# A graph attention layer on one core: the gathered rows weighted in place, one column group of PE per chunk, one gate per batch

## The chip, the cores and the metric

The kernel runs on one core of a Trainium2 chip. The time is that of one execution on the device, in microseconds (us); the figure for a kernel is the median of several runs. The profile is of one execution and has its own time, which stands beside its span below. The engines are PE (matrix multiply), DVE (vector), ACT (activations and copies), POOL (here the issuer of gathers) and SP (issuer of other DMAs).

## The reference

There are N = 12,500 nodes with 128 features and E = 412,500 edges, sorted by target, each with 64 features. `h` is the layer-normed, rectified `x`. For four heads of 32 columns:

```python
h = (node_features @ W_node.T).reshape(num_nodes, H, HD)
e = (edge_features @ W_edge.T).reshape(num_edges, H, HD)
att = jnp.sum(jnp.concatenate([h[src], h[tgt], e], -1) * a, axis=-1)
att = jnp.where(att > 0, att, 0.2 * att)
m = jnp.maximum(segment_max(att, tgt), 0.0)
ex = jnp.exp(att - m[tgt])
denom = segment_sum(ex, tgt) + (num_edges - deg)[:, None] * jnp.exp(-m)
h_prime = segment_sum((ex / denom[tgt])[:, :, None] * h[src], tgt)
return x + h_prime
```

So for every edge a row of `h` is fetched by its source, weighted by a softmax weight, and added up at its target.

## The kernel before, in words

A first stage, of some 112 us, makes a table of rows in HBM, one for each node. A row has `ROW` = 140 floats: four parts of the attention logit that depend on the source, four that depend on the target (`FH` = 8 in all), and for each head its 32 values of `h` and a one (`HB` = 33 floats). The columns come from one matrix, `wall`. For 128 nodes at a time, three such blocks together, ACT copies the product out of PSUM and ACT's queue writes it to the table (`keep_rows`).

The edges are cut into chunks of 896 (`CE`): seven tiles (`T`) of 128 edges, one edge per partition. Eight chunks (`CB`) make a batch, and there are 58 batches, the last with five chunks. Since the edges are sorted, the targets of one chunk lie in a window of 32 nodes (`W`), from the first target on. Per batch:

- `load` lets SP fetch the edge features (`eft`), the targets and eight small slices of the table (`twb`), and names the buffer `hs`, of which there are two, for 56 tiles of 128 rows.
- `gather` has POOL issue one indirect DMA for each of the 56 tiles: 128 rows of the table, chosen by `src`, go to `hs`. The tiles are taken in the order of t, for each t chunk by chunk.
- `weigh` takes the first four columns of `hs` by a stream transpose on DVE (`zst`), adds them to the logits in PSUM (`z`), finds the maximum in each segment by two scans, and leaves the weights `ex` and the maxima `mx` in PSUM, edges on partitions.
- `scatter` goes chunk by chunk. ACT copies `mx` into a buffer `rhs` (three take turns), DVE writes the product of the gathered values and `ex` into it, and PE multiplies it by `hot`, the 0/1 matrix of edge against target. Three tiles (`G` = 3) are done in one matmul, 96 rows of result by 420 columns, of which only the three diagonal blocks of 32 by 140 are wanted; the seventh tile is one of 32 by 140. The result `pa` has one bank for each of two chunks. `keep` lets ACT copy the three blocks to `pas` in SBUF, three copies per chunk, one chunk behind.
- `begin` prepares the next batch: the masks on DVE (`mem`, `key`, `hot`), and `z` on PE from the edge features and `twb`.
- `collect` adds the three blocks and turns them from (row) to (head, row) by partition, in four matmuls with `rsame`, and ACT copies the result into `r`.
- Every second batch, `merge` joins the sums of 16 chunks to the accumulator `acc` on DVE; where a part of the nodes is complete, `finish` divides and adds `x`, and SP stores it.

The order of all this is written out by hand: each engine follows the program's order. In turn b of the main loop come, one after another, `load` and the first part of `gather` for batch b + 1, then `weigh` and `scatter` of b, `begin` of b + 1, `collect` of b, and perhaps `merge` and `finish`. The gathers of b + 1 go into the buffer that batch b - 1 used. They are issued in three parts, cut by `STOPS = (0, 18, 37)`. Ahead of a part stands a gate: a copy of one column on POOL, from something that another engine writes.

```python
if sums is not None:
    nc.gpsimd.tensor_copy(gate[:sums.shape[0], :], sums)
```

The first part's gate reads `r` of batch b - 1. The other two are set inside `scatter`, by `follow`: after the sums of chunk 1, and after those of chunk 5, of batch b itself. (For the first batch there are no gates, and none ahead of the first part of the second.)

After the main loop a further stage, `window`, handles chunks whose targets do not fit one window. It is a loop whose count is worked out from the data.

Of the kernel before, what the change touches and what calls it, by code (L numbers as in the profile page):

```python
# [10 lines left out]
F32 = mybir.dt.float32  # L11
BF16 = mybir.dt.bfloat16
I32 = mybir.dt.int32
AF = mybir.ActivationFunctionType
OP = mybir.AluOpType
# [3 lines left out]
P = 128  # L19
# [4 lines left out]
H = 4  # L24
HD = D // H
T = 7
CE = T * P
CT = 2 * T
NCH = -(-E // CE)
LAST = -(-(E - (NCH - 1) * CE) // P)  # L30
SB = 4
# [5 lines left out]
G = 3  # L37
# [3 lines left out]
W = 32  # L41
NB = -(-N // P)
# [4 lines left out]
FH = 2 * H  # L47
HB = HD + 1
ROW = FH + H * HB
R = CB * H  # L50
NQT = P // R
STOPS = (0, 18, 37)
AW = HD + 3
BUF = max(CE, MC * 2 * AW, CB * H * AW)
# [5 lines left out]
def tiles_of(sc):  # L60

    return [T if c < NCH - 1 else max(LAST, G) for c in (2 * sc, 2 * sc + 1) if c < NCH]


def filled(sc):

    return [T if c < NCH - 1 else LAST for c in (2 * sc, 2 * sc + 1) if c < NCH]
# [23 lines left out]
def kernel(  # L91
# [61 lines left out]
    rhs_bufs = []  # L153
    for i in range(3):
        r = const.tile([P, T, H, AW], F32, name=f"rhs{i}")
        nc.gpsimd.memset(r[:, :, :, HD + 1:], 1.0)
        rhs_bufs.append(r)
# [16 lines left out]
    with (  # L174
# [36 lines left out]
        wall_h = wall[:, FH:].rearrange("p (h k) -> p h k", h=H)  # L211
        nc.vector.memset(wall, 0.0)
        nc.vector.tensor_copy(wall_h[:, :, :HD], pw.rearrange("p (h d) -> p h d", h=H))
        pa = pps.tile([P, FH], F32, name="pw", bufs=1)
        nc.tensor.matmul(pa, wn, a_diag[:, 0:2, :].rearrange("p j h -> p (j h)"), start=True, stop=True)
        nc.vector.tensor_copy(wall[:, :FH], pa)
# [97 lines left out]
        def keep_rows(u):  # L314
            nc.scalar.copy(u.rows, u.ph[:, :u.m, :])
            nc.vector.memset(u.rows[:, :, FH:].rearrange("p b (h k) -> p b h k", h=H)[:, :, :, HD], 1.0)
            nc.vector.tensor_copy(tn[:, u.b0:u.b0 + u.m, :], u.ph[:, :u.m, H:FH])
            if u.last:
                b0, n, rows = u.last
                nc.scalar.dma_start(table[b0 * P:(b0 + n) * P, :].rearrange("(b p) c -> p b c", p=P),  # L320
                                    rows[:, :n, :])
# [91 lines left out]
    def load(s):  # L413

        c0 = s.b * CB
        s.eft = work.tile([P, SB, CE], F32, name="eft")
        nc.sync.dma_start(s.eft, ef[s.b * SB:(s.b + 1) * SB, :, :].rearrange("j p e -> p j e"))
        s.mem = work.tile([P, 2, CE], F32, name="mem")
        for k in range(2):
            rows = dstc[c0 + 4 * k:c0 + 4 * k + 4, :]  # L420
            nc.sync.dma_start(s.mem[:, k, :].bitcast(I32), rows[:, None, :].to_broadcast([4, W, CE]))
        _, at = nc.values_load_multi_w_load_instructions(
            least_i[0:1, c0:c0 + CB], engines=[ENG.SP], min_val=0, max_val=NB * P - W,
            skip_runtime_bounds_check_because="a dst is at most N, and N + W at most NB * P")
        for i, v in enumerate(at):
            r = (i % 4) * W
            nc.sync.dma_start(twb[r:r + W, s.b % 2, i // 4, i * H:(i + 1) * H], table[ds(v, W), H:FH])
        s.hs = work.tile([P, SB * CT, ROW], F32, name="hs", bufs=2)
        s.tiles = []
        for t in range(T):  # L430
            for sc in range(s.b * SB, (s.b + 1) * SB):
                held = filled(sc) + [0, 0]
                for c in range(2):
                    i = (sc - s.b * SB) * CT + c * T + t
                    if t < held[c]:
                        s.tiles.append(i)
                    else:
                        nc.vector.memset(s.hs[:, i, :], 0.0)

    def gather(s, stop, sums=None):  # L440

        if sums is not None:
            nc.gpsimd.tensor_copy(gate[:sums.shape[0], :], sums)  # L443
        i0 = STOPS[stop]
        i1 = STOPS[stop + 1] if stop + 1 < len(STOPS) else len(s.tiles)
        for i in s.tiles[i0:i1]:
            nc.gpsimd.indirect_dma_start(  # L447
                out=s.hs[:, i, :], out_offset=None, in_=table[:, :],
                in_offset=bass.IndirectOffsetOnAxis(ap=s.src[:, i:i + 1], axis=0))
# [39 lines left out]
    def weigh(s):  # L489
# [4 lines left out]
                            s.hs.rearrange("p (q t) k -> p t q k", t=T)[:, :, :, :H])  # L494
# [25 lines left out]
    def scatter(s, follow):  # L520


        last = None
        for j in range(SB):
            sc = s.b * SB + j
            for c, n in enumerate(tiles_of(sc)):
                q = 2 * j + c
                rhs = rhs_bufs[(2 * sc + c) % 3]
                nc.scalar.copy(rhs[:, :n, :, HD + 2], s.mx[:, :n, q * H:(q + 1) * H])  # L529
                i0 = j * CT + c * T  # L530
                nc.vector.tensor_tensor(  # L531
                    rhs[:, :n, :, :HB], s.hs[:, i0:i0 + n, FH:].rearrange("p t (h d) -> p t h d", h=H),
                    s.ex[:, :n, q * H:(q + 1) * H, None].to_broadcast([P, n, H, HB]), op=OP.mult)
                pa = ps.tile([P, G * H * AW], F32, name="pa", bufs=2)

                order = [*range(0, n - G, G), n - G] if n % G == 0 else [0, n - n % G, *range(G, n - n % G, G)]
                for i in order:
                    w = min(G, n - i)
                    nc.tensor.matmul(pa[:w * W, :w * H * AW],  # L539
                                     s.hot[j][:, c * T + i:c * T + i + w, :].rearrange("p t r -> p (t r)"),  # L540
                                     rhs[:, i:i + w, :, :].rearrange("p t h k -> p (t h k)"),
                                     start=(i == order[0]), stop=(i == order[-1]))
                if last is not None:
                    keep(s, *last)
                    if last[0] % 2:
                        follow(last[0] // 2)
                last = (q, pa)
        keep(s, *last)

    def keep(s, q, pa):  # L550
        for g in range(G):
            rows = slice(g * W, (g + 1) * W)
            nc.scalar.copy(s.pas[rows, q, :], pa[rows, g * H * AW:(g + 1) * H * AW])  # L553
# [3 lines left out]
    def collect(s):  # L557

        n = s.chunks
        t2 = ps.tile([P, CB, AW], F32, name="t2")  # L560
        for h in range(H):
            nc.tensor.matmul(t2[h * W:(h + 1) * W, :n, :], rsame[:G * W, :], s.pas[:G * W, :n, h * AW:(h + 1) * AW],
                             start=True, stop=True, tile_position=(0, h * W))
        k = s.b % MB
        if k == 0:
            merged["r"] = work.tile([P, AW, MC + 1], F32, name="r")
        at = 1 + k * CB
        nc.scalar.copy(merged["r"][:, :, at:at + n], t2[:, :n, :].rearrange("p c d -> p d c"))  # L568

    def merge(g, n):  # L570
# [34 lines left out]
        here = ps.tile([P, MC, 2], F32, name="t2")[:, :n, :]  # L605
# [15 lines left out]
    def count_windows():  # L621
# [13 lines left out]
        row = ps.tile([1, NC2], F32, name="t2")  # L635
# [72 lines left out]
    with tc.manual_schedule():  # L708
        for b in range(-1, NBT):
# [6 lines left out]
            if b + 1 < NBT:  # L716
                load(batch(b + 1))
                if b >= 1:
                    at = 1 + (b - 1) % MB * CB
                    gather(batch(b + 1), 0, merged["r"][:, 0, at:at + 1])  # L720
                else:
                    for k in range(len(STOPS) if b < 0 else 1):
                        gather(batch(b + 1), k)
            if b >= 0:
                s = batch(b)
                weigh(s)
                if b + 1 < NBT:
                    load_pen(batch(b + 1))
                for store in stores:
                    store()  # L730
                stores.clear()
                s.pas = work.tile([P, BUF], F32, name="m")[:, :CB * H * AW].rearrange("p (c k) -> p c k", c=CB)

                def follow(j):
                    if b + 1 < NBT and j in (0, 2):
                        gather(batch(b + 1), 1 + j // 2, s.pas[:G * W, 2 * j + 1, 0:1])

                scatter(s, follow)
# [21 lines left out]
    def window():  # L760
# [59 lines left out]


# [44 lines left out]
        for c in range(2):  # L866
            nc.vector.tensor_tensor(z[:, c * T:(c + 1) * T, :], pzt[:, :, c * H:(c + 1) * H],
                                    hs[:, c * T:(c + 1) * T, :H], op=OP.add)
# [56 lines left out]
        for c in range(2):  # L925
            nc.scalar.activation(rhs_bufs[c][:, :, :, HD], att[:, c * T:(c + 1) * T, :], AF.Exp)
# [3 lines left out]
        for c in range(2):  # L930
            t = slice(c * T, (c + 1) * T)
            rhs = rhs_bufs[c]
            nc.vector.tensor_tensor(rhs[:, :, :, :HD],
                                    hs[:, t, FH:].rearrange("p t (h d) -> p t h d", h=H)[:, :, :, :HD],
                                    rhs[:, :, :, HD:HD + 1].to_broadcast([P, T, H, HD]), op=OP.mult)
            for i in range(T):
                k = i % 4
                nc.tensor.matmul(pa[k * W:(k + 1) * W, c, :], hot[:, c * T + i, :],
                                 rhs[:, i, :, :].rearrange("p h k -> p (h k)"),
# [62 lines left out]
```

## Time and profile before

| | |
|---|---|
| Median of three runs | 4299.8 us (4298.55 to 4304.43) |
| The profiled execution | 4299.55 us, its span 4297.8 us |
| Granted PE clock, mean | 0.693 of full speed |
| Busy: POOL | 3107.8 us, 72% |
| Busy: DVE, PE, ACT | 42%, 41%, 17% |
| First gather, last gather | start at 112.85, at 4239.94 us |
| HBM traffic | 417.15 MB read, 15.09 MB written |
| Gathers' queue | 103,136 packets, 231.23 MB, 20.9% of the 16 DMA engines' time |

Busy time is what an engine spent in instructions; the profile does not count registers, semaphores and the issuing of DMAs as busy. Each gather is one instruction on POOL. "Releaser" is what ended a stretch of idle time; "issue" means that nothing the profile shows did. In the names, `m<-pa` is the copy to `pas`, `exr` the bank of `ex` and `mx`, `t<-m,rsame` the matmuls of `collect`, `up` a bank that several steps use in turn.

### The profile page before, as it was taken

Reading aid. Unit: us, or ns where it says so; the run is one execution under the profiler, and the core shown is the slowest. Engines: PE = TensorE matmul, PEld = TensorE weight load, DVE = VectorE, ACT = ScalarE, POOL = GpSimd, SP = SyncE. Lnnn points to the kernel's source line nnn. Section 1 sums busy time; section 2 is a strip of 40 time slices with the busy share of each in tenths; the row PEclk is TensorE's granted clock in tenths of the full one; section 3 lists DMA queues with packets and bytes.
Section 4 is the critical chain, followed back from the end, with each engine's and each line's share of the span. In section 5 each row is a group of like instructions: output and inputs, shape, how many; then the busy total and the mean of one; then the engine's idle time right before and its main releaser. Section 6 shows DMA issues by size and latency. Waiting matters only on the chain.

```text
span 4297.8 us, 25217 instructions
## 1 busy us (share of the span) xinstructions
PE 1767.8 (41%) x5421; PEld 572.8 (13%) x5421; DVE 1788.9 (42%) x3449; ACT 746.4 (17%) x2606; POOL 3107.8 (72%) x3417
## 2 busy tenths in 40 slices
PE   6234344343434443434343434343434343434343
PEld 4011111111111111111111111111111111111111
DVE  7233443344333433443334334443343344433444
ACT  5011111111111111111111111111111111111111
POOL 2777777777777777777777777777777777777773
PEclk8576767676767676767676767676767676767676
DMA  5333433333333333333333333333333333333331
GB/s 159 108 110 84 123 94 110 89 114 85 114 89 109 94 109 89 113 85 114 89 110 93 110 89 112 87 114 90 109 94 109 90 113 85 112 91 110 93 110 36
DMA packets 243603, 434.17 MB, mean 101 GB/s; under 512 B 93914, under 2 KB 144086, under 8 KB 243446
## 3 DMA queue, kind: packets, MB, share of 16 engines
q0 software_dynamic: 103136, 231.23, 20.9%
q1 hardware_dynamic: 126486, 192.44, 13.8%
q10 hardware_dynamic: 13824, 8.82, 0.7%
q8 instruction: 47, 0.77, 0.1%
q14 instruction: 110, 0.90, 0.1%
HBM read 417.15 MB, written 15.09 MB: 101 GB/s over the span
## 4 chain that ended last, share of the span: by engine, by line
POOL 45%; issue 18%; DVE 14%; PE 9%; ACT 6%; DMA 5%; DVEq 0%; POOLq 0%; ACTq 0%
POOL hs L447 44%; PE pa L539 9%; DMA hs<-table,src 5%; DVE up L505 3%; DVE m L507 3%; ACT both L511 2%; DVE z L501 2%; ACT a L502 2%; DVE rhs L531 2%; DVE z L503 1%; DVE a L508 1%; DVE exr L517 1%; ACT m L553 1%; DVE zst L493 1%; POOL gate L443 0%
## 5 line engine op out<-in xcount | busy, mean ns | idle before, releaser
L447 POOL DMA_INDIRECT hs<-table,src x3223 | 3052.6, 947 | 1060.8 <-issue 1058.0
L539 PE MATMUL pa<-rhs,hot 128*96 128x420 f32 (+1 forms) x2762 | 1092.5, 519 | 2216.8 <-DVE rhs L531 2216.3
L531 DVE TENSOR_TENSOR rhs<-hs,exr 128x924 f32<-128x924 f32 x461 | 514.9, 1117 | 608.2 <-ACT rhs L529 608.2
L539 PEld LDWEIGHTS pa<-rhs,hot 128*96 128x96 f32 (+1 forms) x2762 | 333.3, 159 | 2968.6 <-issue 2693.8
L493 DVE STREAM_TRANSPOSE zst<-hs 128x224 f32<-128x224 f32 x58 | 23.9, 411 | 1356.2 <-DMA hs<-table,src 1356.2
L553 ACT COPY m<-pa 32x140 f32<-32x140 f32 x1383 | 367.3, 266 | 762.8 <-PE pa L539 752.1
L465 PE MATMUL z<-eft,wa 128*32 128x384 f32 (+1 forms) x928 | 361.6, 543 | 23.3 <-DMA twb<-table 23.3
L502 ACT ACTIVATE a<-z 32x224 f32<-32x224 f32 x232 | 80.3, 346 | 1539.2 <-DVE z L501 1539.2
L468 PE MATMUL z<-mem,twb 128*32 128x512 f32 x464 | 186.1, 544 | 5.1 <-DMA twb<-table 5.1
L511 ACT ACTIVATE both<-a 32x224 f32<-32x224 f32 x232 | 89.9, 388 | 375.0 <-DVE a L508 370.7
L465 PEld LDWEIGHTS z<-eft,wa 128*32 128x32 f32 x928 | 97.7, 110 | 283.0 <-issue 283.0
L684 PE MATMUL up<-a,ident 128*32 128x224 f32 (+2 forms) x480 | 45.2, 555 | 214.8 <-DVE a L677 214.8
L484 DVE TENSOR_TENSOR hot<-exr,key 128x448 f32<-128x448 f32 x231 | 128.1, 617 | 2.4 <-DVE key L477 0.5
L501 DVE TENSOR_TENSOR z<-z,zst 32x224 f32<-32x224 f32 x232 | 89.8, 387 | 79.9 <-ACT a L502 73.1
L619 DVE TENSOR_TENSOR acc<-acc,a 128x70 f32 x461 | 108.4, 235 | 34.6 <-DVE acc L619 19.8
L529 ACT COPY rhs<-exr 128x28 f32<-128x28 f32 x461 | 96.4, 209 | 132.3 <-DVE rhs L531 68.7
L507 DVE TENSOR_TENSOR_SCAN m<-pen,up 32x896 f32<-32x896 f32 x58 | 116.5, 2008 | 6.7
L505 DVE TENSOR_TENSOR_SCAN up<-pen,z 32x896 f32<-32x896 f32 x58 | 117.0, 2017 | 2.0
L568 ACT COPY r<-t 128x280 f32<-128x280 f32 (+1 forms) x58 | 23.7, 408 | 506.1 <-PE z L468 505.5
L580 DVE TENSOR_SCALAR mc<-r 128x16 f32<-128x16 f32 (+1 forms) x29 | 6.1, 209 | 229.3 <-ACT r L568 229.3
L513 DVE SCALAR_TENSOR_TENSOR both<-pen,m 32x224 f32<-32x224 f32 x232 | 90.2, 389 | 2.4
L460 DVE TENSOR_SCALAR mem<-mem,nid 128x896 f32<-128x896 int32 x116 | 74.7, 685 | 21.9 <-issue 16.2
(140 smaller groups left out, 1037.8 us busy)
## 6 DMA issues: line engine op xcount, KB each, us to landing
eft<-in_ef SPq DMA_DIRECT2D x58, 1792.0 KB
mem<-in_dstc SPq DMA_DIRECT2D x116, 448.0 KB
hs<-table,src POOLq DMA_INDIRECT x3223, 2.6
twb<-table SPq DMA_DIRECT2D x464, 0.5 KB
pen<-pens SPq DMA_DIRECT2D x58, 112.1 KB
table<-rows ACTq DMA_DIRECT2D x10, 630.0 KB
xg<-in_x SPq DMA_DIRECT2D x14, 448.0 KB
out<-xg SPq DMA_DIRECT2D x13, 448.0 KB
```

The costliest lines, as they stand in the source:

```text
L447: nc.gpsimd.indirect_dma_start(out=s.hs[:, i, :], out_offset=None, in_=table[:, :], in_offset=bass.IndirectOffsetOnAxis(ap=s.src[:, i:i + ...
L465: nc.tensor.matmul(s.z[:, part], wa3[:, j, :], s.eft[:, j, part], start=(j == 0), stop=False)
L468: nc.tensor.matmul(s.z[:, part], twb[:, s.b % 2, k, :], s.mem[:, k, part], start=False, stop=(k == 1))
L484: nc.vector.tensor_tensor(hot, rows_ps[:, None, :].to_broadcast([P, CT, W]), key[:, j * CT:(j + 1) * CT, None].to_broadcast([P, CT, W]), o ...
L501: nc.vector.tensor_tensor(grouped(s.z, g), grouped(s.z, g), zst[g * R:(g + 1) * R, :, :], op=OP.add)
L502: nc.scalar.activation(grouped(att, g), grouped(s.z, g), AF.Identity, scale=0.2)
L505: nc.vector.tensor_tensor_scan(up, s.pen[:, :CE], s.z, 0.0, op0=OP.add, op1=OP.max)
L507: nc.vector.tensor_tensor_scan(m[:, ::-1], s.pen[:, CE:0:-1], up[:, ::-1], 0.0, op0=OP.add, op1=OP.max)
L511: nc.scalar.activation(both[g * R:(g + 1) * R, 0, :, :], grouped(att, g), AF.Exp)
L531: nc.vector.tensor_tensor(rhs[:, :n, :, :HB], s.hs[:, i0:i0 + n, FH:].rearrange("p t (h d) -> p t h d", h=H), s.ex[:, :n, q * H:(q + 1) * ...
L539: nc.tensor.matmul(pa[:w * W, :w * H * AW], s.hot[j][:, c * T + i:c * T + i + w, :].rearrange("p t r -> p (t r)"), rhs[:, i:i + w, :, :].r ...
L553: nc.scalar.copy(s.pas[rows, q, :], pa[rows, g * H * AW:(g + 1) * H * AW])
```

## The change

The layout of the table changes: a row has, for each head, 32 values, two ones and the logit's source part (`AW` = 35 floats), then the four target parts: `EROW` = 140, `ROW` = 144. So a gathered row already has the shape of PE's operand. In `scatter`, ACT copies `mx` over the logit column of `hs`, for all chunks at first; DVE multiplies the first 33 columns of each head by `ex` in place; and PE takes `hs` itself as its moving operand, one tile of 140 columns at a time. Each chunk has a column group of PE, hence 32 partitions of the result, by its number modulo 4 (`G` is now 4); two chunks take turns. The result of all eight chunks is one bank, `s.pa`.

`keep`, `follow`, `rhs_bufs`, `STOPS` and the matmuls of `collect` are gone. `collect` instead has ACT move each group and head straight from PSUM to `r`, sixteen copies per batch. Ahead of these it writes one column, `sums`, which the only gate of a batch reads: the gathers of batch b + 1 are issued in one part, behind the end of PE's work for batch b - 1.

```diff
-G = 3
+G = P // W
-FH = 2 * H
-ROW = FH + H * HB
-STOPS = (0, 18, 37)
 AW = HD + 3
+HB = HD + 1
+EROW = H * AW
+ROW = EROW + H
...
-    rhs_bufs = []
-    for i in range(3):
-        r = const.tile([P, T, H, AW], F32, name=f"rhs{i}")
-        nc.gpsimd.memset(r[:, :, :, HD + 1:], 1.0)
-        rhs_bufs.append(r)
+    sums = const.tile([P, 1], F32, name="sums")
...
-            nc.vector.memset(u.rows[:, :, FH:].rearrange("p b (h k) -> p b h k", h=H)[:, :, :, HD], 1.0)
-            nc.vector.tensor_copy(tn[:, u.b0:u.b0 + u.m, :], u.ph[:, :u.m, H:FH])
+            nc.vector.memset(u.rows[:, :, :EROW].rearrange("p b (h k) -> p b h k", h=H)[:, :, :, HD:HD + 2], 1.0)
+            nc.vector.tensor_copy(tn[:, u.b0:u.b0 + u.m, :], u.ph[:, :u.m, EROW:])
...
-            nc.sync.dma_start(twb[r:r + W, s.b % 2, i // 4, i * H:(i + 1) * H], table[ds(v, W), H:FH])
+            nc.sync.dma_start(twb[r:r + W, s.b % 2, i // 4, i * H:(i + 1) * H], table[ds(v, W), EROW:])
...
-    def gather(s, stop, sums=None):
+    def gather(s, sums=None):
         if sums is not None:
-            nc.gpsimd.tensor_copy(gate[:sums.shape[0], :], sums)
-        i0 = STOPS[stop]
-        i1 = STOPS[stop + 1] if stop + 1 < len(STOPS) else len(s.tiles)
-        for i in s.tiles[i0:i1]:
+            nc.gpsimd.tensor_copy(gate, sums)
+        for i in s.tiles:
             nc.gpsimd.indirect_dma_start(
...
-                            s.hs.rearrange("p (q t) k -> p t q k", t=T)[:, :, :, :H])
+                            s.hs[:, :, :EROW].rearrange("p (q t) (h k) -> p t q h k", t=T, h=H)[:, :, :, :, AW - 1])
...
-    def scatter(s, follow):
+    def scatter(s):
+        s.pa = ps.tile([P, CB // G, H * AW], F32, name="pa", bufs=2)
+        by_chunk = s.hs[:, :, :EROW].rearrange("p (q t) (h k) -> p q t h k", t=T, h=H)
+        for q in range(s.chunks):
+            nc.scalar.copy(by_chunk[:, q, :, :, AW - 1], s.mx[:, :, q * H:(q + 1) * H])
         for j in range(SB):
+            tiles = list(enumerate(tiles_of(s.b * SB + j)))
+            for c, n in tiles:
+                q = 2 * j + c
+                rows = by_chunk[:, q, :n, :, :HB]
+                nc.vector.tensor_tensor(
+                    rows, rows, s.ex[:, :n, q * H:(q + 1) * H, None].to_broadcast([P, n, H, HB]), op=OP.mult)
+            for i in range(T):
+                for c, n in tiles:
+                    if i < n:
+                        q = 2 * j + c
+                        g = q % G
+                        nc.tensor.matmul(s.pa[g * W:(g + 1) * W, q // G, :], s.hot[j][:, c * T + i, :],
+                                         s.hs[:, q * T + i, :EROW],
+                                         start=(i == 0), stop=(i == n - 1), tile_position=(0, g * W))
...
     def collect(s):
         n = s.chunks
-        t2 = ps.tile([P, CB, AW], F32, name="t2")
-        for h in range(H):
-            nc.tensor.matmul(t2[h * W:(h + 1) * W, :n, :], rsame[:G * W, :], s.pas[:G * W, :n, h * AW:(h + 1) * AW],
-                             start=True, stop=True, tile_position=(0, h * W))
+        if s.b + 2 < NBT:
+            nc.scalar.copy(sums, s.pa[:, CB // G - 1, 0:1])
...
-        nc.scalar.copy(merged["r"][:, :, at:at + n], t2[:, :n, :].rearrange("p c d -> p d c"))
+        for g in range(min(n, G)):
+            to = merged["r"][:, :, at + g:at + n:G]
+            for h in range(H):
+                nc.scalar.copy(to[h * W:(h + 1) * W, :, :],
+                               s.pa[g * W:(g + 1) * W, :-(-(n - g) // G), h * AW:(h + 1) * AW]
+                               .rearrange("p c d -> p d c"))
...
-                if b >= 1:
-                    at = 1 + (b - 1) % MB * CB
-                    gather(batch(b + 1), 0, merged["r"][:, 0, at:at + 1])
-                else:
-                    for k in range(len(STOPS) if b < 0 else 1):
-                        gather(batch(b + 1), k)
+                gather(batch(b + 1), sums if b >= 1 else None)
...
-                def follow(j):
-                    if b + 1 < NBT and j in (0, 2):
-                        gather(batch(b + 1), 1 + j // 2, s.pas[:G * W, 2 * j + 1, 0:1])
```

`wall` and `window` follow the new layout; a bank that was named `t2` in two other places is now `here`.

More of the change, by code (lines that the diff above doesn't have):

```diff
@@ L46 @@
 XS = 3
-FH = 2 * H
-HB = HD + 1
-ROW = FH + H * HB
 R = CB * H
 NQT = P // R
-STOPS = (0, 18, 37)
 AW = HD + 3
+HB = HD + 1
+EROW = H * AW
+ROW = EROW + H
 BUF = max(CE, MC * 2 * AW, CB * H * AW)
@@ L60, in tiles_of @@
 def tiles_of(sc):
-    return [T if c < NCH - 1 else max(LAST, G) for c in (2 * sc, 2 * sc + 1) if c < NCH]
-def filled(sc):
     return [T if c < NCH - 1 else LAST for c in (2 * sc, 2 * sc + 1) if c < NCH]
@@ L210 @@
         nc.tensor.transpose(pw, wn, ident)
-        wall_h = wall[:, FH:].rearrange("p (h k) -> p h k", h=H)
+        wall_h = wall[:, :EROW].rearrange("p (h k) -> p h k", h=H)
         nc.vector.memset(wall, 0.0)
         nc.vector.tensor_copy(wall_h[:, :, :HD], pw.rearrange("p (h d) -> p h d", h=H))
-        pa = pps.tile([P, FH], F32, name="pw", bufs=1)
+        pa = pps.tile([P, 2 * H], F32, name="pw", bufs=1)
         nc.tensor.matmul(pa, wn, a_diag[:, 0:2, :].rearrange("p j h -> p (j h)"), start=True, stop=True)
-        nc.vector.tensor_copy(wall[:, :FH], pa)
+        nc.vector.tensor_copy(wall_h[:, :, AW - 1], pa[:, :H])
+        nc.vector.tensor_copy(wall[:, EROW:], pa[:, H:])
         pe = pps.tile([P, H], F32, name="pw", bufs=1)
@@ L431, in load @@
             for sc in range(s.b * SB, (s.b + 1) * SB):
-                held = filled(sc) + [0, 0]
+                held = tiles_of(sc) + [0, 0]
                 for c in range(2):
@@ L518, in weigh @@
                                 both[:, k, :, :].rearrange("p t r -> p (t r)"))
-    def scatter(s, follow):
-        last = None
+    def scatter(s):
[3 more added lines that the diff above has]
+            nc.scalar.copy(by_chunk[:, q, :, :, AW - 1], s.mx[:, :, q * H:(q + 1) * H])
         for j in range(SB):
-            sc = s.b * SB + j
-            for c, n in enumerate(tiles_of(sc)):
+            tiles = list(enumerate(tiles_of(s.b * SB + j)))
+            for c, n in tiles:
@@ L527, in scatter @@
                 q = 2 * j + c
-                rhs = rhs_bufs[(2 * sc + c) % 3]
-                nc.scalar.copy(rhs[:, :n, :, HD + 2], s.mx[:, :n, q * H:(q + 1) * H])
-                i0 = j * CT + c * T
+                rows = by_chunk[:, q, :n, :, :HB]
                 nc.vector.tensor_tensor(
-                    rhs[:, :n, :, :HB], s.hs[:, i0:i0 + n, FH:].rearrange("p t (h d) -> p t h d", h=H),
-                    s.ex[:, :n, q * H:(q + 1) * H, None].to_broadcast([P, n, H, HB]), op=OP.mult)
@@ L534, in scatter @@
[L534 to L553, printed above, removed]
+                    rows, rows, s.ex[:, :n, q * H:(q + 1) * H, None].to_broadcast([P, n, H, HB]), op=OP.mult)
@@ L604, in merge @@
         put = work.tile([P, BUF], F32, name="a")[:, :MC * 2 * AW].rearrange("p (c j d) -> p c j d", c=MC, j=2)
-        here = ps.tile([P, MC, 2], F32, name="t2")[:, :n, :]
+        here = ps.tile([P, MC, 2], F32, name="here")[:, :n, :]
         nc.vector.tensor_copy(here, lastm[:, c0:c0 + n, :])
@@ L634, in count_windows @@
         nc.vector.tensor_copy(more, far)
-        row = ps.tile([1, NC2], F32, name="t2")
+        row = ps.tile([1, NC2], F32, name="here")
         for g in range(NG):
@@ L731 @@
                 stores.clear()
-                s.pas = work.tile([P, BUF], F32, name="m")[:, :CB * H * AW].rearrange("p (c k) -> p c k", c=CB)
-                def follow(j):
-                    if b + 1 < NBT and j in (0, 2):
-                        gather(batch(b + 1), 1 + j // 2, s.pas[:G * W, 2 * j + 1, 0:1])
-                scatter(s, follow)
+                scatter(s)
             if b + 1 < NBT:
@@ L819, in window @@
                 in_offset=bass.IndirectOffsetOnAxis(ap=src_w[:, t:t + 1], axis=0))
+        hs4 = hs[:, :, :EROW].rearrange("p t (h k) -> p t h k", h=H)
         pst = ps.tile([P, 2], F32, name="pz")
@@ L867, in window @@
             nc.vector.tensor_tensor(z[:, c * T:(c + 1) * T, :], pzt[:, :, c * H:(c + 1) * H],
-                                    hs[:, c * T:(c + 1) * T, :H], op=OP.add)
+                                    hs4[:, c * T:(c + 1) * T, :, AW - 1],
+                                    op=OP.add)
         groups = [(c, f, w, u) for c in range(2) for f, w, u in groups_of(T)]
@@ L925, in window @@
         for c in range(2):
-            nc.scalar.activation(rhs_bufs[c][:, :, :, HD], att[:, c * T:(c + 1) * T, :], AF.Exp)
+            nc.scalar.activation(hs4[:, c * T:(c + 1) * T, :, HD], att[:, c * T:(c + 1) * T, :], AF.Exp)
         pa = ps.tile([P, 2, H * AW], F32, name="pa")
@@ L931, in window @@
             t = slice(c * T, (c + 1) * T)
[L932 to L935, printed above, removed]
+            nc.vector.tensor_tensor(hs4[:, t, :, :HD], hs4[:, t, :, :HD],
+                                    hs4[:, t, :, HD:HD + 1].to_broadcast([P, T, H, HD]), op=OP.mult)
             for i in range(T):
@@ L938, in window @@
                 nc.tensor.matmul(pa[k * W:(k + 1) * W, c, :], hot[:, c * T + i, :],
-                                 rhs[:, i, :, :].rearrange("p h k -> p (h k)"),
+                                 hs[:, c * T + i, :EROW],
                                  start=(i < 4), stop=(i + 4 >= T), tile_position=(0, k * W))
```

## The prediction

> **What bounds the kernel now.** I read the page's engine table and its groups first, then the chain of waits, then POOL's and PE's timelines over one batch, then the last 100 us.
>
> ```profile
> PE 1767.8 (41%) x5421; PEld 572.8 (13%) x5421; DVE 1788.9 (42%) x3449; ACT 746.4 (17%) x2606; POOL 3107.8 (72%) x3417
> ...
> L447 POOL DMA_INDIRECT hs<-table,src x3223 | 3052.6, 947 | 1060.8 <-issue 1058.0
> ```
>
> POOL's 3223 gathers are busy 947 ns each, and the idle time before them is put down to no releaser ("issue"). POOL's timeline (start, duration, what, idle before it and releaser) shows the pace and its breaks:
>
> ```profile
> 2050.05 0.20 POOL L443 COPY gate<-r 128x1 f32<-128x1 f32 x1
> 2050.41 0.98 POOL L447 DMA_INDIRECT hs<-table,src  x1 [0.15 <-issue]
> ...
> 2071.66 0.94 POOL L447 DMA_INDIRECT hs<-table,src  x1 [0.30 <-issue]
> 2073.70 0.18 POOL L443 COPY gate<-m 96x1 f32<-96x1 f32 x1 [1.09 <-ACT m L553]
> 2074.38 0.97 POOL L447 DMA_INDIRECT hs<-table,src  x1 [0.51 <-issue]
> ...
> 2097.91 0.20 POOL L443 COPY gate<-m 96x1 f32<-96x1 f32 x1
> 2098.26 0.97 POOL L447 DMA_INDIRECT hs<-table,src  x1 [0.15 <-issue]
> ```
>
> Seventy-two undisturbed starts between 114.31 and 204.17 us lie 1.248 us apart. A gate that need not wait stretches one such step by about 0.085 us. The gate at 2073.70 waits for ACT's copy of the sums of chunk 1: 2.72 us between gathers instead of 1.248, and with 0.03 on the next, 1.50 us lost. Batch to batch (2050.41 to 2122.06) is 71.65 us = 56 x 1.248 = 69.89, + 2 x 0.085, + 1.50, + 0.1 for odd gathers of 1.02 us.
>
> Why that gate is late is told by the chain of waits, one turn of which reads (start, us, what; only the longest pieces):
>
> ```profile
> 2049.11 2.49 DMA hs<-table,src
> 2055.42 1.10 DVE z L503
> 2056.55 2.03 DVE up L505
> 2058.66 2.02 DVE m L507
> 2060.71 1.09 DVE a L508
> 2064.70 1.13 DVE rhs L531
> 2065.96 6.76 PE pa L539 x12
> 2074.38 0.97 POOL hs L447
> ```
>
> The last row of batch b lands, `weigh` takes 12.7 us (2051.72 to 2064.43), the first two chunks 9 us more, the gate opens, and 38 gathers of batch b+1 (47.7 us) must follow before the next `weigh`: 71.65 again. The two bounds are only 1.5 us apart: this loop, and POOL's own 70. The loop takes the first of them.
>
> **The change, part by part.**
>
> *Gates.* 114 copies `gate<-m` go; 56 stay, on `sums`. Batch b+1 then needs only its buffer, hence the end of PE in batch b-1. That is due when POOL finishes the 56 gathers of batch b: 2050.05 + 70 = 2120 for the scatter that starts at 2064. Saved per batch 1.50 + 0.085, 56 times up to the last batch but one: 88.8 us; the first gate was later (204.17 to 207.40), 0.5 more. What is late next is POOL itself. Gathers before 207 us ran through 72 in a row with no gate, so the long run is not a new state.
>
> *Gather of 576 B instead of 560 B.* Queue 0's share of the DMA engines (20.9%) grows by 3%, and nothing waits for that: landing is 2.6 us. POOL's 0.944 us has one size only in this trace. Lower bound 0 (no row gets shorter); upper bound, all proportional to bytes, 2.9% of 0.944 = 27 ns x 3223 = 87 us, the whole gain. The trace doesn't choose. The Trainium skill (DMA: Bandwidth & Descriptors, section Terms) calls a descriptor a 16-byte record that tells one engine to move N bytes: its writing would cost the same for any N. By the bytes the time would be 4300, by the page 4213; I take 0, since the number of rows is the same 128, and keep the other end as a rival.
>
> *Product on DVE.* The same 461 instructions of 1117 ns, now into `hs`, with the same one PSUM operand: 0. The `rhs` buffers' turn-taking goes (DVE idles 608.2 us before L531), off POOL's path. The stream transpose reads `z` at a stride of 35: 411 ns, at most twice that, under the slack below.
>
> *ACT copies of `mx`.* 461 of 209 ns as before, but a batch's eight now come first: 8 x 0.209 = 1.7 us ahead of the first product if DVE waits for all.
>
> *PE.* 48 instructions per batch (32 of 420 columns, 16 of 140) become 112 of 140: 15,680 columns both ways, 64 more weight loads. The trace prices a 32-column load on the rows of `begin` (start of each load):
>
> ```profile
> 2088.85 0.11 PEld L465 LDWEIGHTS z<-eft,wa 128*32 128x32 f32 x1 [0.32 <-issue]
> 2089.28 0.11 PEld L465 LDWEIGHTS z<-eft,wa 128*32 128x32 f32 x1 [0.32 <-issue]
> ...
> 2090.67 0.11 PEld L465 LDWEIGHTS z<-eft,wa 128*32 128x32 f32 x1 [0.21 <-issue]
> 2090.99 0.11 PEld L465 LDWEIGHTS z<-eft,wa 128*32 128x32 f32 x1 [0.21 <-issue]
> ```
>
> Steps of 0.43 us for 512 columns and 0.32 for 384 are 0.84 ns per column with nothing left for the load. So 140 columns are 0.118 us, 112 of them 13 us, as now. Against the change speaks the skill (TensorE: Matmul & The Clock Gate, Part 3: Packing small matmuls): a load overlaps running matmuls only where the row group differs, and here all four column groups use all rows. Then it is 112 x (0.118 + 0.110) = 25.5 us. The worst that rows give is the 140-column group at its mean in this window, 0.327, with 0.116 for the load: 0.443 x 112 = 49.6 us. PE starts at about 2064.4 + 1.7 + 2 x 1.12 = 2068.4 and ends at 2082, 2094 or 2118: before 2120 each time. The sum is the same by row and by rule; I take 20 us, between the first two. This cover is what costs the PE edit at nothing; each us beyond it would be half a us per batch, since the buffer comes round every second batch.
>
> *Moving the sums.* Gone per batch: 24 copies of 266 ns (6.4 us) and one of 408 on ACT, 8 matmuls of `collect` which stood on PE behind `begin` (9 us). New: one `sums` and 16 copies of 32x70, between the 209 ns of a 28-element copy and the 266 of 140: 0.23 x 16 = 3.7 us. `sums` stands ahead of the sixteen, so POOL doesn't wait for them; behind them on ACT is the next `weigh`, behind them on DVE is `merge`. With `merge` and `finish` DVE now ends at 2043.1 and idles 8.6 us before the next transpose; `merge` starts after scatter + 4.5 us instead of + 10, so it is not later for a scatter up to 5 us longer.
>
> *SP and preparation.* No DMA is added on SP or ACT; the loads of the next batch are let go by `begin` on PE, some 60 us ahead of use, which covers them. `wall` and the rows grow from 140 to 144 columns: ACT's copy of 128x420 (0.49 us) by 3% over 33 units, +0.5 us. POOL's memsets lie in its 82.7 us idle before the first gather.
>
> *Tail.* The last batch has 31 gathers, so there PE is late, not POOL: `begin` ends at 4245.9, its rows came by 4242.7, and the gain of gates within it is not counted above. A scatter of 20 us in place of 19 shifts it by +1 to +3; five chunks' first products wait for 5 copies and two products instead of one, +2; no buffers to wait for, -3; sixteen small copies for 2.6 us of copies and matmuls, +1. I take +2, between -4 and +25.
>
> **The sum.** 4299.55 (the profiled execution: span 4297.8 and 1.75 around it; 0.25 under the median 4299.8) - 88.8 - 0.5 + 0.5 + 2 = 4212.7, so 4213.
>
> **The rivals.**
> - *POOL pays by the byte* (no change): +87 us, 4300. For it: nothing in the trace excludes it. Against: 128 rows in each gather as before. 7 in 100, and some part of it inside the range.
> - *Waits on the gathers* (slower). Each gather now overwrites rows that PE, DVE and ACT used, not DVE alone, so POOL may stop to look at more signals. Price: the gap behind a gate that had to wait is 0.50 instead of 0.30, 0.2 us per look; place: gathers of batches 2 to 57. It turns to a loss from 8 such looks per batch (1.6 us); at 20 it costs 4 us x 56 = 224, so 4437. Against: the first eight gathers after the gate at 2050.05, which follow DVE's eight products, start 1.25 us apart: a wait that is long over costs nothing there. 6 in 100.
> - *PE becomes the bound* (slower): from 0.455 us per matmul `sums` comes after 2120; from 0.485 the round of two batches is longer than 143.3 us; at 0.6 it is 155 us, +6 per batch, near 4640. Against: 0.443 is the worst the rows give. 3 in 100.
> - *The change doesn't do what it says*: the first gate may be met by no stall at all and another wait (landing, SP's loads) hold POOL at 71.6: 4295 to 4300. 2 in 100.
>
> **How the numbers follow.** POOL alone as the bound, 82 in 100, from 4195 (the tail's best, 6 lower, no odd gathers, 6, and the 5 us between first and last gather, 4127.9, that these steps leave unexplained) to 4245 (the tail's worst). The range goes to 4260 to take in a third or half of the price by bytes or a few looks per batch. What this kernel's measurement can tell from no change is about 0.2%, 8.6 us. Faster by more: 0.86, the main case and the milder ends of the rivals; the same 0.05; slower 0.09, which is the waits and PE.
>
> **What would show it.** Gathers 1.248 us apart through a whole batch, batch to batch 70.0 to 70.1; 56 copies `gate<-sums` of about 0.2 us with no idle time before them; POOL's mean of a gather still 947; PE's `pa` 112 per batch, over within 25 us of its first. The chain of waits should be POOL for over nine tenths between 260 and 4110 us. It would be wrong if a gather grows by 10 ns or more, if gaps of 0.5 us stand between gathers, or if the gate waits for ACT.

## The result, and the profile after

The changed kernel takes 4203.41 us (median of 4 runs, 4202.70 to 4204.16) where the kernel before takes 4301.25 (4 runs, 4298.55 to 4304.43). The ratio is 0.9772, with a 95% interval of 0.9755 to 0.9789: faster by 2.3%. The profiled execution took 4202.7 us, its span is 4200.5 (before 4299.55 and 4297.8). The forecast was 4213, in a range of 4195 to 4260.

The page's engine table and the groups of POOL and of PE's scatter after the change (the columns of a group: line, engine, operation, tiles, count | busy us, mean ns | idle before it, and what ended it):

```profile
PE 1108.4 (26%) x8641; PEld 623.1 (15%) x8641; DVE 1758.2 (42%) x3450; ACT 564.9 (13%) x2149; POOL 3086.6 (73%) x3300
...
L436 POOL DMA_INDIRECT hs<-table,src x3223 | 3053.0, 947 | 1056.3 <-issue 1056.3
L527 PE MATMUL pa<-hs,hot 128*32 128x140 f32 x6446 | 493.0, 338 | 2838.9 <-DVE hs L520 2809.3
...
L545 ACT COPY r<-pa 32x70 f32<-32x70 f32 x928 | 252.8, 272 | 27.3 <-PE pa L527 17.2
L537 ACT COPY sums<-pa 128x1 f32<-128x1 f32 x56 | 8.9, 159 | 580.7 <-PE pa L527 580.7
```

The gathers are as many and as long as before, 947 ns, though each fetches 16 bytes more per row. (The trace has two matmul records for each matmul of the program, so a scatter of 56 tiles has 112; "matmul" below means a record.) POOL's timeline shows a batch from gate to gate:

```profile
2006.21 0.94 POOL L436 DMA_INDIRECT hs<-table,src  x1 [0.30 <-issue]
2007.15 0.20 POOL L434 COPY gate<-sums 128x1 f32<-128x1 f32 x1
2007.51 0.98 POOL L436 DMA_INDIRECT hs<-table,src  x1 [0.15 <-issue]
...
2076.29 0.94 POOL L436 DMA_INDIRECT hs<-table,src  x1 [0.30 <-issue]
2077.23 0.20 POOL L434 COPY gate<-sums 128x1 f32<-128x1 f32 x1
2077.58 0.98 POOL L436 DMA_INDIRECT hs<-table,src  x1 [0.15 <-issue]
```

The only gate follows the gather before it at once. Batch to batch it is 70.08 us here and 70.20 for the next (2147.43), where before it was 71.65. The view of the gate by itself has nothing under its heading of idle time:

```profile
L434 POOL COPY gate<-sums x56: 192/197/203, 253.2 to 4111.8; 128x1 f32<-128x1 f32 x56
its engine sat idle before it (us, times) until:
who waited for it (us, times):
```

So all 56 gates are free, as against 63.4 us of waiting for ACT in 56 of the old ones. The slack can be read from ACT and PE over the same batch: `sums` is written 44 us before the gate at 2077.23 reads it. PE's scatter runs from 2023.73 to 2032.80, 9.1 us.

```profile
2022.56 8.31 DVE L520 TENSOR_TENSOR hs<-hs,exr 128x924 f32<-128x924 f32 x8 [0.88 <-ACT hs L514]
...
2023.73 0.67 PE L527 MATMUL pa<-hs,hot 128*32 128x140 f32 x2 [39.07 <-DVE hs L520]
2024.80 5.94 PE L527 MATMUL pa<-hs,hot 128*32 128x140 f32 x84 [0.40 <-issue]
2030.97 1.47 PE L527 MATMUL pa<-hs,hot 128*32 128x140 f32 x21 [0.23 <-issue]
...
2032.89 0.16 ACT L537 COPY sums<-pa 128x1 f32<-128x1 f32 x1 [10.36 <-PE pa L527]
2032.94 4.55 ACT L545 COPY r<-pa 32x70 f32<-32x70 f32 x16
```

Where the 97.3 us of the span went: the first gather starts at 112.86 (112.85 before); the last at 4149.77 (4239.94), 90.2 us earlier; from there to the end it is 50.7 us (57.9), 7.1 less. The page's chain of waits breaks off some 58 us before the end in this trace, so it can't be used for the share of POOL.

The end is no longer PE's. Before, the last `weigh` had its rows and waited for `z`; after, `begin` on PE ends at 4146.1 (4142.91 + 3.17), ahead of the rows, and DVE waits for these. The last batch of both kernels, from its transpose on, the kernel before first:

```profile
4242.69 0.41 DVE L493 STREAM_TRANSPOSE zst<-hs 128x224 f32<-128x224 f32 x1 [4.54 <-DMA hs<-table,src]
...
4245.94 0.39 DVE L501 TENSOR_TENSOR z<-z,zst 32x224 f32<-32x224 f32 x1 [2.83 <-PE z L468]
...
4258.65 0.21 ACT L529 COPY rhs<-exr 128x28 f32<-128x28 f32 x1 [0.95 <-DVE exr L517]
...
4271.71 1.65 ACT L553 COPY m<-pa 32x140 f32<-32x140 f32 x6 [1.58 <-PE pa L539]
...
4274.35 0.17 DVE L580 TENSOR_SCALAR mc<-r 128x13 f32<-128x13 f32 x1 [3.46 <-ACT r L568]
```

and the changed one:

```profile
4142.91 3.17 PE L457 MATMUL z<-mem,twb 128*32 128x512 f32 x8
4152.59 0.58 DVE L482 STREAM_TRANSPOSE zst<-hs 128x224 f32<-128x224 f32 x1 [13.26 <-DMA hs<-table,src]
...
4165.50 0.61 ACT L514 COPY hs<-exr 128x28 f32<-128x28 f32 x5 [0.95 <-DVE exr L506]
...
4172.97 3.77 ACT L545 COPY r<-pa 32x70 f32<-32x70 f32 x16 [6.87 <-PE pa L527]
4176.78 0.18 DVE L559 TENSOR_SCALAR mc<-r 128x13 f32<-128x13 f32 x1 [5.81 <-ACT r L545]
```

The wait of 2.8 us for `z` is gone; five chunks take 7.5 us (4165.50 to 4172.97) instead of 13.1 (4258.65 to 4271.71), 5.6 less; the way from there to `merge` takes 3.8 us instead of 2.6, 1.2 more. Together 7.2 less.

### The profile page after: what moved, and what is told of

Its sections match the earlier page's. It is cut to its first block, busy times and chain, and to the rows that moved or that the text cites. A ratio compares the mean times of both kernels' runs of the same rounds, so it can differ in the third digit from the quotient of the medians.

```text
span 4200.5 us, 30865 instructions
## 1 busy us (share of the span) xinstructions
PE 1108.4 (26%) x8641; PEld 623.1 (15%) x8641; DVE 1758.2 (42%) x3450; ACT 564.9 (13%) x2149; POOL 3086.6 (73%) x3300
## 3 DMA queue, kind: packets, MB, share of 16 engines
q0 software_dynamic: 103136, 237.83, 23.4%
## 5 line engine op out<-in xcount | busy, mean ns | idle before, releaser
L527 PE MATMUL pa<-hs,hot 128*32 128x140 f32 x6446 | 493.0, 338 | 2838.9 <-DVE hs L520 2809.3
L482 DVE STREAM_TRANSPOSE zst<-hs 128x224 f32<-128x224 f32 x58 | 33.6, 579 | 2004.0 <-DMA hs<-table,src 2004.0
L527 PEld LDWEIGHTS pa<-hs,hot 128*32 128x32 f32 x6446 | 408.7, 132 | 2947.4 <-DVE hs L520 2850.3
L520 DVE TENSOR_TENSOR hs<-hs,exr 128x924 f32<-128x924 f32 x461 | 478.2, 1110 | 50.8 <-ACT hs L514 50.8
L545 ACT COPY r<-pa 32x70 f32<-32x70 f32 x928 | 252.8, 272 | 27.3 <-PE pa L527 17.2
L537 ACT COPY sums<-pa 128x1 f32<-128x1 f32 x56 | 8.9, 159 | 580.7 <-PE pa L527 580.7
L492 DVE TENSOR_TENSOR z<-z,a 32x896 f32<-32x896 f32 x58 | 63.0, 1087 | 23.9 <-ACT a L491 23.9
L457 PEld LDWEIGHTS z<-mem,twb 128*32 128x32 f32 x464 | 51.2, 111 | 133.3 <-issue 110.2
```

Of the source, the lines that this page charges most:

```text
L457: nc.tensor.matmul(s.z[:, part], twb[:, s.b % 2, k, :], s.mem[:, k, part], start=False, stop=(k == 1))
L520: nc.vector.tensor_tensor(rows, rows, s.ex[:, :n, q * H:(q + 1) * H, None].to_broadcast([P, n, H, HB]), op=OP.mult)
L527: nc.tensor.matmul(s.pa[g * W:(g + 1) * W, q // G, :], s.hot[j][:, c * T + i, :], s.hs[:, q * T + i, :EROW], start=(i == 0), stop=(i == n ...
L545: nc.scalar.copy(to[h * W:(h + 1) * W, :, :], s.pa[g * W:(g + 1) * W, :-(-(n - g) // G), h * AW:(h + 1) * AW] .rearrange("p c d -> p d c"))
```

## The experiments

The theory: POOL's gathers, at 1.248 us each, were one bound, and the loop through the gate at chunk 1 another, 1.5 us longer; with the gate gone POOL is alone. The rivals of the prediction: POOL pays by the byte; waits on gathers cost; PE becomes the bound.

Two chips were used. The first three experiments below ran on one where the kernel before takes 4300.26 us, as in the first measurement. The other four ran on one where the same kernel takes 5443.03 us (9 runs, 5421.88 to 5449.45), and their ratios are to that.

**Wider rows.** `ROW = EROW + H + 24`, with the copies into the last columns cut to `EROW:EROW + H`.

```diff
-ROW = EROW + H
+ROW = EROW + H + 24
```

> The changed kernel with 24 floats of padding behind each row of the table: gathers of 672 B instead of 576 B, nothing else reads them. Theory (POOL pays by the row): a gather stays at 947 ns, the step at 1.248 us, and the time at 4203 to 4207. Rival (POOL pays by the byte): 0.944 x 24/144 = 157 ns x 3223 = 507 us more, 4710; a tenth of that would be 4254.

Measured 4209.20 us (2 runs), ratio 0.9786 (0.9758 to 0.9815) to the kernel before: some 2 us above the theory's 4207, and far below the rival's 4710 and 4254.

```profile
L436 POOL DMA_INDIRECT hs<-table,src x3223: 942/946/1264, 114.1 to 4155.6; - x190
```

The columns are shortest, median and longest ns, and first and last start. A gather has a median of 946 ns where the changed kernel has 944. From first to last gather it is 4041.5 us instead of 4036.9: 4.6 us for 96 bytes a row, so some 0.8 us for the 16 that the change adds. POOL pays by the row; the rival of 87 us is out. The other 1.2 us lie before the first gather.

**One chunk at a time on PE.** The two loops inside `scatter` are exchanged.

```diff
-            for i in range(T):
-                for c, n in tiles:
+            for c, n in tiles:
+                for i in range(T):
```

> The changed kernel with the two chunks of a pair one after the other on PE instead of turn by turn. Theory (0.07 us per matmul comes from two column groups at work at once): a scatter takes PE 112 x 0.118 to 0.14, that is 13 to 16 us instead of 9.1; the time 4203 to 4207, since POOL has the slack and only the tail's five chunks show. Rival (a matmul of 140 columns takes 0.07 us by itself): 9.1 us stay, 4203.

Measured 4208.17 us (2 runs), ratio 0.9784 (0.9756 to 0.9812). PE's timeline:

```profile
2025.58 11.79 PE L527 MATMUL pa<-hs,hot 128*32 128x140 f32 x109 [35.25 <-DVE hs L520]
2037.10 0.62 PE L454 MATMUL z<-eft,wa 128*32 128x512 f32 x1
2037.21 0.52 PE L527 MATMUL pa<-hs,hot 128*32 128x140 f32 x3
```

The scatter takes 12.15 us, just under the 13 to 16 expected, where turn by turn it is 9.1; the rival, 9.1 either way, is out. The mean, 0.108 us per matmul, is not the pace of one column group, since PE's clock changes on the way:

```profile
2025.50:2029.20 3.70, 3.62 (x20) 0.50 0.58 156
2030.00:2037.00 7.00, 7.00 (x84) 1.00 0.24 55
```

A row gives a stretch of time, its length, PE's busy time in scatter's matmuls, how many of these lie in the stretch or reach into it, the granted clock, and what the DMA engines did. In the first stretch the matmuls of one column group start 0.233 us apart, in the second 0.119. Where a chunk ends and the next begins in another column group a few run side by side, so 14 matmuls take 1.22 us. It costs POOL no wait, and all 56 gates are free; the time from the last gather to the end grows from 50.7 to 53.4 us, since the last five chunks take 10.3 us instead of 7.5. (The last gather comes 3.2 us later as well: the gathers are 3.3 us longer in sum, though their median is still 944 ns. Why is open.) That puts the time 1 us above the 4207 expected at most.

**Seven times the matmuls.**

```diff
-            for i in range(T):
+            for k, i in itertools.product(range(REP), range(T)):
...
-                                         start=(i == 0), stop=(i == n - 1), tile_position=(0, g * W))
+                                         start=(k == 0 and i == 0), stop=(k == REP - 1 and i == n - 1),
+                                         tile_position=(0, g * W))
```

> The changed kernel with every matmul of the scatter issued seven times into the same sums (the sums, and so the output, are seven times too large in part). The last 28 matmuls of a scatter took 1.9 us, 0.07 us each, so the scatter should take PE 7 x 112 x 0.07 = 55 us. By the prediction's condition (only the release of the buffer counts, due 70 us after the gathers end) sums come 16.6 + 55 = 71.6 us after, 1.6 us late for every second batch: 0.8 x 57 = 45 us more, 4250. Rival (weigh, scatter and the next batch's begin form a loop that must fit into one batch, since weigh needs z): 13 + 3.1 + 55 + 9.3 + 0.5 = 81 us per batch, 10.8 x 57 = 615 us more, 4815.

Measured 4660.68 us (2 runs), ratio 1.0836 (1.0805 to 1.0868) to the kernel before. Neither number holds. (The sums of this kernel come out seven times too large.) The scatter takes PE 47.7 us, not 55: 784 matmuls at 0.061. All but the first 3.3 us of it run at the full clock, and there two matmuls, one in each of two column groups, start every 0.119 us, the pace of one in the kernel above.

```profile
2062.40:2065.70 3.30, 2.88 (x22) 0.50 0.29 68
2067.00:2109.00 42.00, 42.00 (x730) 1.00 0.23 53
...
2062.42 0.68 PE L528 MATMUL pa<-hs,hot 128*32 128x140 f32 x2 [22.91 <-DVE hs L521]
2063.49 46.29 PE L528 MATMUL pa<-hs,hot 128*32 128x140 f32 x776 [0.40 <-issue]
...
2115.55 3.17 PE L458 MATMUL z<-mem,twb 128*32 128x512 f32 x8
2132.99 0.68 PE L528 MATMUL pa<-hs,hot 128*32 128x140 f32 x2 [14.28 <-DVE hs L521]
```

By the prediction's condition 16.6 + 47.7 = 64 us would be in time, and the kernel no slower than 4203; by the rival's loop the turn is 73.6. A turn from scatter to scatter measures 70.6 us where there is no `merge` (above), 79.9 where there is one (1982.54 to 2062.42), and 86.2 with a `finish` too (2132.99 to 2219.20). So the loop of weigh, scatter and `begin` is what binds, not the release of the buffer, and in every second batch it is longer than the rival said: DVE's masks `hot` wait for PE to be done with the old ones, `merge` stands behind them on DVE, and the next `weigh` behind `merge`.

```profile
2030.98 0.62 DVE L474 TENSOR_TENSOR hot<-exr,key 128x448 f32<-128x448 f32 x1 [10.61 <-PE pa L528]
...
2046.32 1.05 DVE L600 TENSOR_TENSOR acc<-acc,a 128x70 f32 x4 [0.20 <-DVE acc L600]
2047.49 0.58 DVE L483 STREAM_TRANSPOSE zst<-hs 128x224 f32<-128x224 f32 x1
```

From the end of the scatter to the next transpose that is 16.5 us. Without `merge` the transpose is done early, and the step after it waits for `begin`, until 8.6 us after the scatter. POOL is held only as a consequence: 36 of the 56 gates wait, 333.6 us in all, of the 457 us that the kernel takes more than the changed one.

**On the other chip: the changed kernel again.**

> The changed kernel itself beside the three others, as their mark: 4203 within 3 us, 56 gates without idle time.

Measured 5304.96 us (5 runs), ratio 0.9744 (0.9731 to 0.9757): the change gains 2.6% here too, but by another way. The time on this chip is not POOL's pace: gathers are 946 ns. PE's timeline has stretches of single matmuls, with no releaser named:

```profile
2012.29 0.39 PE L527 MATMUL pa<-hs,hot 128*32 128x140 f32 x1 [2.41 <-issue]
2014.39 0.39 PE L527 MATMUL pa<-hs,hot 128*32 128x140 f32 x1 [1.71 <-DMA hs<-table,src]
2017.19 0.39 PE L527 MATMUL pa<-hs,hot 128*32 128x140 f32 x1 [2.41 <-issue]
...
2036.78 4.84 PE L527 MATMUL pa<-hs,hot 128*32 128x140 f32 x47 [0.31 <-issue]
...
2042.68 0.18 POOL L434 COPY gate<-sums 128x1 f32<-128x1 f32 x1 [14.38 <-ACT sums L537]
```

From 1999 to 2033 us PE starts one matmul in 2.1 or 2.8 us; POOL's last gather of the batch starts at 2027.35; some 6 us later the gaps on PE begin to close, and from 2036.78 it is back at its pace. The scatter takes some 50 us, and all 56 gates wait, 1036.6 us in all. Neither the expected 4203 nor the free gates were seen here. What holds PE is not shown; that its instructions arrive late while gathers flow would fit.

**On the other chip: the kernel before with one gate.**

```diff
-STOPS = (0, 18, 37)
+STOPS = (0,)
...
-                    if b + 1 < NBT and j in (0, 2):
-                        gather(batch(b + 1), 1 + j // 2, s.pas[:G * W, 2 * j + 1, 0:1])
+                    return
```

> The kernel before with the two gates inside its scatter taken away and nothing else: gathers in one part per batch, behind the sums of the batch before last. Theory (the gate at chunk 1 held POOL, and its removal is the gain): 56 x (1.50 + 0.085) + 0.5 = 89 us less, 4210, batch to batch 70.1. It keeps the old tail (57.9 us from the last gather's start to the end, where the changed kernel has 50.7), so it stays about 7 us above the changed kernel. Rival (the shorter path of scatter and collect is the gain, gates don't matter): 4290 to 4300.

Measured 5842.49 us (5 runs), ratio 1.0731 (1.0716 to 1.0746): slower by 7%, against both expectations. PE's timeline:

```profile
2080.54 2.15 PE L539 MATMUL pa<-rhs,hot 128*96 128x420 f32 x6 [0.45 <-issue]
2094.15 3.94 PE L539 MATMUL pa<-rhs,hot 128*96 128x420 f32 x6 [11.46 <-issue]
2110.25 3.94 PE L539 MATMUL pa<-rhs,hot 128*96 128x420 f32 x6 [12.16 <-issue]
2127.05 3.94 PE L539 MATMUL pa<-rhs,hot 128*96 128x420 f32 x6 [12.86 <-DVE rhs L531]
```

In such a stretch a chunk takes 10 to 17 us instead of 2.2, while gathers flow without a break, and the gate, behind `collect`, waits 1568 us in all for ACT, DVE and a load. This does not answer what the edit does on the chip of the first measurement, where it wasn't run: in the traces from there PE has no such stretches. The size of the gate's share rests on the traces of the two kernels alone.

**On the other chip: the changed kernel with three gates.** The gathers are cut at 0, 18 and 37 as before, behind a copy by ACT after the first and the third pair of chunks.

```diff
+            if s.b + 1 < NBT and j in (0, 2):
+                nc.scalar.copy(part, s.pa[:2 * W, j // 2, 0:1])
+                gather(batch(s.b + 1), (1 + j // 2,), part)
```

> The changed kernel with the gathers cut into three parts again at 0, 18 and 37, gates behind the PE sums of the first and the third pair of chunks of the batch in work. Theory (a gate costs what its wait costs): the first pair is through PE some 5 us after the weights are there instead of 9, so the loop is 38 gathers 47.7 + landing 1.7 + weigh 13.5 + scatter 5 = 68, under POOL's own 70; no gate waits, and 113 more gates of 0.085 cost 9.6 us: 4213. Rival (the removed gates as such are the gain): the stall of 1.5 us per batch is back, 4285 to 4295.

Measured 5348.00 us (5 runs, 5320.89 to 5376.86), ratio 0.9810 (0.9788 to 0.9831), 43 us more than the changed kernel there. Gates do wait on this chip (57 for `part`, 777.8 us, and 51 for `sums`, 326.7; in the changed kernel 56, 1036.6), and PE's slow stretches are there too; so the question whether they would be free with PE at its pace stays open. The trace of the changed kernel argues that they would: 18 gathers from 2007.51 end at 2030, and the first pair's 28 matmuls are over by about 2027.7.

**On the other chip: no gate.**

```diff
-                gather(batch(b + 1), sums if b >= 1 else None)
+                gather(batch(b + 1))
```

> The changed kernel without any gate and without the copy of sums: the first gather of a batch itself waits for PE, DVE and earlier gathers. Theory (a gate that need not wait costs 0.085 us, a wait that is long over nothing): 56 x 0.085 = 4.8 us less, 4198. Rival (several waits on one gather cost 0.2 us each, which the gate took off it): 3 x 0.2 x 56 - 4.8 = 29 us more, 4232.

Measured 5297.23 us (5 runs, 5294.15 to 5301.35), ratio 0.9731 (0.9718 to 0.9744) beside the changed kernel's 0.9744 (0.9731 to 0.9757). The edit leaves ACT's copy of `sums` in place, though the expectation has it gone; nothing reads it. One run of the changed kernel (5299.06) lies among these, so the 7.7 us, 0.15%, are a hint and no more. The rival's 29 us more was not seen: on this chip a first gather that itself looks at several signals costs no more than the gate did. So this kernel is faster than the kernel before, by 2.7%, and not clearly faster than the changed one.

## Why the prediction was right

*The gates.* The sum said 88.8 us for 56 gates and 0.5 for the first, and 1.6 more in the last batch that would not count. The last gather starts 90.2 us earlier, with gathers of the same length and no gate that waits. This is read from two traces, not from an edit of the gates alone on that chip. The change also shortens the way to the first sums, and by the trace that alone could have freed the gate at chunk 1: with the old cut of the gathers it would come at about 2030, and the first pair's matmuls end at about 2027.7. Which of the two is the gain was not measured apart. A turn was to be 70.0 to 70.1 us and is 70.08 to 70.20.

*The gather's size.* The value 0 was right within a microsecond; what it is per byte, the trace of before could not tell and the wide rows did. Queue 0's share of the DMA engines was to grow by 3% and went from 20.9% to 23.4%; nothing waited for it.

*PE.* This is the term that was mis-sized. The prediction took 20 us and it is 9.1. It stood between 13 by the rows of `begin` and 25.5 by the rule of the Trainium skill (TensorE: Matmul & The Clock Gate, Part 3: Packing small matmuls) that a load overlaps running matmuls only where the row group differs. The rule did not hold here: at the full clock matmuls of one column group start 0.119 us apart, with their loads, which is what `begin`'s rate gives for 140 columns (0.118), so nothing is left for a load. The row was right for one column group; both left out that two column groups work at once, a pair in 0.119 us. They left out the clock too: in the batch shown it is at 0.50 for the first 3.7 us, which makes 0.119 into 0.233. In the changed kernel the last chunks also wait for DVE's eight products, 8.31 us. Since the cover was wide, the nearness of the total says nothing for this term: a scatter of up to some 30 us would have cost POOL nothing before the last batch.

*The tail.* +2 was said, between -4 and +25. From the last gather on it is -7.1; of the span's 97.3 us the 89.3 of the sum's gates leave 8.0, so by the sum's own terms it is -8.0, 10 us from what was said and below the range given for it. It is the wrong term again: with PE at 9.1 us `begin` is early, and the last five chunks take 5.6 us less. This and the preparation, 0 instead of 0.5, make up the distance from 4213 to 4203. The sixteen copies went the other way: 272 ns each, not 230, as long as the old ones of 140 elements (266), though they move half as many.

*The rivals.* By the byte: out. Waits on gathers: not seen, either in the first batch after a gate or without it. PE as the bound: its place and point were wrong. The prediction let it decide at 0.455 us per matmul by the release of the buffer and counted 0.443 as safe; the seven-fold kernel shows that the loop through `begin`, `weigh` and, every second time, `merge` decides, from a scatter of about 47 us in plain batches and less where there is a `merge`. The slack is smaller than the prediction said. As an estimate from these turns, less their 47.7 us of scatter, a turn stays within POOL's 70.1 us up to a scatter of 47 us in a plain batch, 38 with a `merge` and 32 with a `finish` too: three to five times the scatter as it is.

## What to carry to other kernels

When an engine is nearly saturated, compare the turn of each loop that goes through its waits with its own pace: a wait of 1.5 us that ends a long loop is worth its size and no more, because the engine's own pace is next. Before a stage is called hidden, go round every loop that it lies on, with what stands behind it in the order of each engine, not the one loop of the edit. And a gate that costs time where everything flows can be of use on a chip where it does not; on one such chip taking it out alone cost 7%, while the whole change gained.

## What the hardware showed that was not expected

- Matmuls of 140 columns with 128 rows start 0.119 us apart in one column group, loads included, at a granted clock of 1.00; when two column groups take turns, a pair starts every 0.119 us.
- Every scatter begins at a granted clock of 0.50. In the kernel before that covers most of the first two chunks, on which the gate waited: their 12 matmuls take 6.76 us, the 12 of the next two 4.09. The difference, 2.7 us, is more than the 1.50 lost at the gate; how much of it is the clock was not measured apart.

```profile
2065.90:2071.50 5.60, 5.54 (x10) 0.50 0.54 142
...
2075.10 4.09 PE L539 MATMUL pa<-rhs,hot 128*96 128x420 f32 x12 [0.45 <-DVE rhs L531]
```

- 96 bytes more per gathered row cost 2 ns of POOL per 128 rows, though the packets of that queue rose from 103,136 to 154,704.
- On one chip PE started single matmuls 2.1 or 2.8 us apart for some 35 us of a batch, only while gathers flowed, and the same kernel took 5443 instead of 4300 us. The cause stays open.
